# First group of the second layer's scans: its preparation spread over four more PSUM banks, and ScalarE's table loads moved

## The chip, the core and the metric

The kernel runs on one core of a Trainium2 chip. Five engines work side by side, each with an instruction queue of its own that it executes in order: TensorE (PE, matrix products; PEld is its weight load), VectorE (DVE), ScalarE (ACT, copies and functions from tables), GpSimd (POOL), and SyncE (SP), whose queue here issues transfers. They wait for one another by semaphores. Data lie in SBUF (128 partitions); TensorE writes to PSUM, which has eight banks of 512 float32 per partition. The metric is the time of one execution on the device in microseconds (us), the median of several runs.

## The reference

Two layers of the same build are applied to an image of 64 x 64 pixels with 96 channels. Each adds to x the output of a group norm, a projection to 2 x 192 channels (x_val and the gate z), a 3 x 3 depthwise convolution with silu, four selective scans with 16 states per channel along four pixel orders, a layer norm, the gate and a projection back. Cut to what matters, with the second layer's scan:

```python
xz = x @ in_proj_w.T;  xin, z = split(xz)
xc = silu(depthwise_conv3x3(xin) + conv_b)          # called u below
xs = stack([xf, xf[::-1], xf[o1], xf[o2]])          # four orders of the pixels
x_dbl = einsum('bkdl,kcd->bkcl', xs, x_proj_weight)
dts = einsum('bkrl,kdr->bkdl', x_dbl[:, :, :6], dt_projs_weight)
Bs, Cs = x_dbl[:, :, 6:22], x_dbl[:, :, 22:]
A = -exp(A_logs)
delta = softplus(dts + delta_bias)
def step(h, t):                                     # over 4096 pixels
    h = h * exp(d_t[..., None] * A) + (d_t * u_t)[..., None] * B_t[:, :, None, :]
    y = einsum('bkdn,bkn->bkd', h, C_t)
    return h, y
y = ys + u * D
y = layernorm(sum of the four, back in pixel order) * silu(z)
return y @ out_proj_w.T
```

The first layer's scan is written with cumulative sums, and its state is negligible some rows away from the image's border.

## The kernel before

The 4096 pixels of a channel lie in two halves over the 128 partitions: `u[T]` and `y[T]` (T = 0, 1, 2) are tiles of 128 x 2048, in which partitions 0 to 63 hold one half of the pixels of 64 channels and partitions 64 to 127 the other half. A *chunk* c is 512 columns of such a tile, that is 1024 pixels.

Each layer runs through the same stages. `head` (from L1005 on) computes the statistics of the group norm (`gst`, Ln at L1034 and Exp at L1035 on ScalarE), normalizes x (`xn`, L1040), projects it (`in`, copied to `pad` at L1051), runs the nine taps of the convolution on VectorE (`acc`, L1099 and L1101) and the silus on ScalarE (L1082 for the gate `sz`, L1103 for `u`). `scan_weights` is called ahead of `head`: it loads the projection weights (`xw`), those of delta (`dwb`) and log A (`ab`) over SP's queue, and computes `am` = -exp(log A) and half of it, with two exponents on ScalarE (L218) and two products on VectorE (L219, L220) for each pair of directions. The buffers of pair 0 have one copy for both layers.

In the first layer `near_scans` handles the pixels near the border, then reads a flag that says whether the rest can be left out. A branch (L1231) on it skips `far_scans`; in the profiled execution it was skipped. Its part up to the scans is prepared by TensorE, ScalarE and VectorE in turn (`nu`, `npj`, `npd`), and its transfers are `nC`, `ncb` and `ndu` on SP and `dt`, `S` on ScalarE's queue.

In the second layer `scans` does the work. There are 16 groups (two pairs of orders, two directions, four chunks). Each has 24 units: three tiles T by eight state pairs m. For each unit ScalarE computes a = exp(delta x A) (`stage_a`), TensorE makes b, which holds B times delta u, in PSUM, VectorE runs the scan h over 1024 pixels (`stage_s`), POOL multiplies by C (`stage_c`, hc), and TensorE adds the product up over the states (`stage_r`, ys). For even m, b comes from a selection of B's rows by TensorE (`stage_B`, selh, bank pair "b0") that VectorE multiplies by du (`stage_b`); for odd m it comes from products bT of transposed delta u and transposed B made by ScalarE, which TensorE transposes back (`stage_t`, "b1").

`prelude(k)` lists the preparation of group k as steps with a slot in units, group k's own first unit being slot 24. `project(h)` projects half h of the chunk to 124 rows (B three times, the six rows of each delta, C) as `pj`; `projected(h)` copies them to `xd` and takes B in bfloat16 (B3), and `less_part` and `next_part` subtract that from the rest and take the next two parts, so that three bfloat16 parts make up B. `rows` writes C to DRAM, from where `fetch_c` spreads its rows (cb). `tokens_B` transposes B (tB, copied to BT). `delta(T)` makes softplus: a product pd, then on ScalarE su = |pd|, sp = relu, w = exp(-su), ln = log(1+w), pd = 1 + w, then four VectorE steps (from group 1 on only the first, the other three on POOL) which leave delta in sp and delta times u in su. `spread(T)` copies both over SP's queue to the layout of the scan (dt, du). `tokens_du(e)` transposes su (tu, copied to duT), and `product` makes bT.

All PSUM tiles of the prelude share one bank, tag "v"; the other seven are "y0", "y1", "y2" (ys, one each), "b0" and "b1" (two each). So each step of the prelude that takes a bank waits until the one before it is read. The steps with a time below zero, all of group 0's and those of group 1's with a slot below 0, are issued ahead of the loop, sorted by time over both groups. Until the loop begins a scheduler may rearrange them; from `pinned` on the order written is kept. Calls to `tc.keep_in_program_order` pin single instructions, the table loads among them.

`tail` (from L1137 on) takes the four chunks from the last to the first through `centre` (mean by TensorE, subtraction on VectorE, Square on ScalarE), `scale` (variance by TensorE, Ln at L1159 and Exp at L1160, four VectorE operations g) and `project`, one chunk behind the other.

All operations of `scans` are recorded at L646, the line of its helper, and are told apart by their tiles.

Of the kernel before, what the change touches and what calls it, by code (L numbers as in the profile page):

```python
# [8 lines left out]
F32 = mybir.dt.float32  # L9
# [11 lines left out]
NS = 16  # L21
# [22 lines left out]
def two_ss2d_layers(  # L44
# [132 lines left out]
    def scan_weights(l):  # L177

        xw, dwb, am = [], [], []
        D = 1 + l
        for p in range(1 + l):
            lp = 2 * l + p
            w = swp.tile([128, 2, 3, NC], F32, tag=f"xw{p}", name=f"xw{lp}")
            v = swp.tile([128, 2, 3, 128], F32, tag=f"dwb{p}", name=f"dwb{lp}")
            e = swp.tile([128, 2, 3, NS + 1], F32, tag=f"ab{p}", name=f"ab{lp}")
            a = swp.tile([128, 2, 2, 3, NP], F32, tag=f"am{p}", name=f"am{lp}")
            nc.vector.memset(v[96:128, 0:D], 0.0)
            for d in range(D):  # L190
                r = slice(NB + RK * d, NB + RK * d + RK)
                rr = slice(RK * d, RK * d + RK)
                hi = slice(64 * d, 64 * d + 64)
                c0 = NB + 2 * RK + NS * d
                for half in HALF:
                    for to, of in ((slice(0, NC - NS), slice(0, NC - NS)), (slice(NC - NS, NC), slice(c0, c0 + NS))):
                        nc.sync.dma_start(
                            out=w[half, d, 0:2, to],
                            in_=xpw[lp, :, d, of].rearrange("(b p) c -> p b c", b=2),
                        )  # L200
                        nc.sync.dma_start(out=w[half, d, 2, to], in_=xpw[lp, hi, 2, of])
                    nc.sync.dma_start(
                        out=v[r, d, 0:2, half], in_=dtw[lp, rr, d, :].rearrange("r (b p) -> r b p", b=2)
                    )
                    nc.sync.dma_start(out=v[r, d, 2, half], in_=dtw[lp, rr, 2, hi])
                    for b, (of, q) in enumerate(((HALF[0], d), (HALF[1], d), (hi, 2))):
                        nc.sync.dma_start(
                            out=v[NC : NC + 1, d, b, half],
                            in_=alb[lp, of, q, NS : NS + 1].rearrange("p o -> o p"),
                        )  # L210
                    nc.sync.dma_start(
                        out=e[half, d, 0:2, :],
                        in_=alb[lp, :, d, :].rearrange("(b p) n -> p b n", b=2),
                    )
                    nc.sync.dma_start(out=e[half, d, 2, :], in_=alb[lp, hi, 2, :])

            for h, half in enumerate(HALF):
                nc.scalar.activation(a[half, 0, 0:D], e[half, 0:D, :, h:NS:2], AF.Exp)  # L218
            nc.vector.tensor_scalar_mul(a[:, 1, 0:D], a[:, 0, 0:D], -0.5)  # L219
            nc.vector.tensor_scalar_mul(a[:, 0, 0:D], a[:, 0, 0:D], -1.0)  # L220
            xw.append(w)
            dwb.append(v)
            am.append(a)
        return xw, dwb, am

    def row_of(rows, m, dst):

# [12 lines left out]
    def near_scans(weights):  # L240

        xw, dwb, am = (v[0] for v in weights)
        WN = 4 * NEAR
        with ExitStack() as sc:
            once = sc.enter_context(tc.tile_pool(name="near", bufs=1))
# [87 lines left out]
                once.tile([128, 3, 2, 2 * NEAR], F32, name=f"n{nm}") for nm in ("dt", "du", "S")  # L335
            )
            load_exp_ln()
            for T in range(3):
                nc.scalar.activation(w[:, T], ps[:, T], AF.Abs)
                nc.vector.tensor_scalar_max(v[:, T], ps[:, T], 0.0)  # L340
# [170 lines left out]

    def far_scans(weights):

        xw, dwb, am = (v[0] for v in weights)
        with ExitStack() as sc:
            pre = sc.enter_context(tc.tile_pool(name="fpre", bufs=1))
            mn = sc.enter_context(tc.tile_pool(name="fmn", bufs=2))
# [112 lines left out]
    def scans(weights):  # L630
# [1 line left out]

        xw, dwb, am = weights
        pinned = []

        class Ordered:
# [15 lines left out]
        with ExitStack() as sc:  # L654
# [2 lines left out]
            pps = sc.enter_context(tc.tile_pool(name="pps", bufs=1, space=PSUM))  # L657
            dram = sc.enter_context(tc.tile_pool(name="dram", bufs=3, space=DRAM))
            load_exp_ln()
            carry = pre.tile([128, 3, NP], F32, name="carry")  # L660
            PER = 3 * NP
            LAG = 3
# [3 lines left out]
            xd = pre.tile([128, TC], F32, name="xd")  # L666
            dve.memset(xd[96:128], 1.0)

            def spare(name):

                return pps.tile([128, HT], F32, tag="v", name=name)

            def views(t, c):

# [12 lines left out]
            def prelude(k):  # L687
# [3 lines left out]
                me = state[k]  # L691
                add_engine = pool if k else dve

                def turn(T):

                    t = pre.tile([128, HT // 2], F32, tag="turn", name=f"turn{k}_{T}")
                    v = views(u[T], c)[1][0]
                    t3 = t.rearrange("p (r w) -> p r w", w=HW)
                    act.copy(t3, v)
                    act.copy(v[:, :, ::-1], t3)  # L700

                def project(h):
                    ps = me["ps"] = spare(f"pj{k}_{h}")
                    for T in range(3):
                        pe.matmul(
                            ps[0:NC], xw[p][HALF[h], d, T, :], chunk(u[T], c)[HALF[h]],
# [1 line left out]
                        )  # L708

                def projected(h):  # L710
                    act.copy(xd[0:NC, halves[h]], me["ps"][0:NC])
                    if h == 0:
                        me["B3"] = pre.tile([NB, TC], BF16, tag="B3", name=f"B3{k}", bufs=3)
                    act.copy(me["B3"][:, halves[h]], me["ps"][0:NB])

                def less_part(h):
                    pe.matmul(
                        me["ps"][0:NB], less, me["B3"][:, halves[h]],  # L720
                        start=False, stop=True, skip_group_check=True,
                    )

                def next_part(part, h):
                    q = slice(0, 64 - 32 * part)
                    act.copy(me["B3"][q, halves[h]], me["ps"][q])

                def rows():
                    me["C"] = dram.tile([NS, TC], F32, tag="C", name=f"C{k}")
# [35 lines left out]
                def delta(T):  # L765

                    def begin():
                        ps = me["pd", T] = spare(f"pd{k}_{T}")
                        for h, half in enumerate(HALF):
                            pe.matmul(  # L770
                                ps[half], dwb[p][96 : NC + 1, d, T, half],
# [53 lines left out]
                    steps += [(-17 + T, lambda T=T: turn(T)) for T in range(3)]  # L825
                for h in range(2):
                    o = -13 + 3 * h
                    steps += [
                        (o, lambda h=h: project(h)),
                        (o + 1, lambda h=h: projected(h)), (o + 1, lambda h=h: less_part(h)),  # L830
                        (o + 2, lambda h=h: next_part(0, h)), (o + 2, lambda h=h: less_part(h)),
                        (o + 3, lambda h=h: next_part(1, h)),
                    ]
                steps += [
                    (-9, rows), (-6.8, tokens_B), (-5.95, tokens_B_out),
# [127 lines left out]
            def stage_y(j):  # L963
# [6 lines left out]
                        act.copy(view, f(ps))  # L970

            steps = [
                (PER * (k - 1) + slot, n, step)
                for k in range(len(GROUPS)) for n, (slot, step) in enumerate(prelude(k))
            ]
            steps.sort(key=lambda at: at[:2])
            while steps[0][0] < 0:
                steps.pop(0)[2]()

# [143 lines left out]
    def tail(l, w, xT):  # L1123
# [3 lines left out]
        with ExitStack() as sc:  # L1127
# [4 lines left out]
            for c in order:  # L1132
# [4 lines left out]
                    nc.sync.dma_start(out=t, in_=szd[l][T, :, HT * c : HT * (c + 1)])  # L1137
                cut = slice(TC * c, TC * (c + 1))
                nc.sync.dma_start(out=xT[:, cut], in_=xs[:, cut])
            load_exp_ln()  # L1140
            live = {}

            def centre(c):
# [9 lines left out]
            def scale(c):  # L1153
                cut = slice(HT * c, HT * (c + 1))
                pv = fps.tile([128, HT], F32, tag="v", name=f"v_{l}_{c}", bufs=1)
                for T in range(3):
                    nc.tensor.matmul(pv, pos, live[c, T], start=(T == 0), stop=(T == 2))
                rstd = fin.tile([128, HT], F32, tag="rstd", name=f"rstd{l}_{c}")
                nc.scalar.activation(rstd, pv, AF.Ln, bias=eps5)  # L1159
                nc.scalar.activation(rstd, rstd, AF.Exp, scale=-0.5)  # L1160
                for T in range(3):
# [158 lines left out]
```

## Time and profile before

| | us |
|---|---|
| median of 3 runs (1598.1 to 1598.31) | 1598.23 |
| the profiled execution | 1606.41 |
| its span, first to last instruction | 1604.6 |
| mean granted clock of TensorE | 0.874 of full |
| busy: VectorE / TensorE / ScalarE / POOL | 1392.8 / 1224.2 / 1211.8 / 1092.3 |
| first layer: head and convolution, near scans, tail | 0 to 97, to 194, to 241 |
| second layer: head and convolution, start of the scans, loop, tail | to 320, to 390, to 1556, to 1604.6 |

The times of all views are counted from the span's start. A line of the timeline has the start, the time from the first start to the last end, the engine, the line of the kernel, the operation with its output and inputs, how many instructions are merged in it, and in brackets the idle time of the engine before them with what ended it. A line of waits has the sum, the number and the longest one. A line of windows has the bounds and the length, busy time and number of instructions, TensorE's granted clock, and the share and rate of the transfers. The page's second part cuts the span into 40 slices, each digit being the busy share in tenths.

### The profile page before, as it was taken

How to read it: one execution, taken by the hardware profiler on the slowest of the kernel's cores; microseconds unless marked ns; L12 is line 12 of the kernel's file. 1: busy time of each engine (PE TensorE's matmuls, PEld its weight loads, DVE VectorE, ACT ScalarE, POOL GpSimd, SP SyncE). 2: the span in 40 equal slices, each digit the busy share in tenths (PEclk: the TensorE clock that was granted, in tenths of full speed). 3: DMA queues.
4: the chain of work that ended last, by engine and by line, in shares of the span. 5: the costliest groups of instructions: out<-in, count | busy, mean ns of one | idle time of the engine just before them, and what ended most of it. 6: DMA issues, size and time to landing. Idle time of an engine off the chain costs nothing.

```text
span 1604.6 us, 17094 instructions
## 1 busy us (share of the span) xinstructions
PE 1224.2 (76%) x5014; PEld 487.9 (30%) x5014; DVE 1392.8 (87%) x971; ACT 1211.8 (76%) x2463; POOL 1092.3 (68%) x577
## 2 busy tenths in 40 slices
PE   5452677157888888888878888888888888887768
PEld 3131422013333232333333333333333332322223
DVE  6946577923999999999999999999999999999976
ACT  2534156246898988989899989999898889897743
POOL 0022100003989899898989898998989898989860
PEclk8755598555999999999999899989999998999999
DMA  4304142040263443615262634526252626345323
GB/s 103 90 25 89 33 124 84 9 101 22 65 147 82 104 114 75 153 57 134 55 131 74 138 86 100 121 74 150 53 133 55 139 68 137 90 95 123 87 67 104
DMA packets 84308, 148.10 MB, mean 92 GB/s; under 512 B 31676, under 2 KB 35068, under 8 KB 84108
## 3 DMA queue, kind: packets, MB, share of 16 engines
q1 hardware_dynamic: 80428, 143.76, 37.4%
q10 hardware_dynamic: 3776, 3.15, 0.9%
q8 instruction: 41, 0.67, 0.2%
q14 instruction: 63, 0.52, 0.1%
HBM read 80.85 MB, written 12.13 MB: 58 GB/s over the span
## 4 chain that ended last, share of the span: by engine, by line
DVE 29%; issue 20%; ACT 14%; PE 12%; DMA 6%; SPq 4%; POOL 2%; DVEq 0%; ACTq 0%; POOLq 0%
DVE h L646 16%; DVE b L646 6%; ACT a L646 5%; SPq L646 4%; PE ys L646 4%; DVE acc L1101 4%; ACT bT L646 3%; DMA cb<-C 3%; PE pj L646 3%; PE b L646 2%; PE pd L646 2%; POOL hc L646 2%; DMA xT<-xs 1%; DMA du<-su 1%; DVE w L646 1%
## 5 line engine op out<-in xcount | busy, mean ns | idle before, releaser
L646 POOL TENSOR_TENSOR hc<-h,cb 128x1024 f32<-128x1024 f32 x384 | 903.3, 2367 | 251.6 <-DVE h L646 198.1
L646 DVE TENSOR_TENSOR_SCAN h<-a,carry,b 128x1024 f32<-128x1024 f32 x288 | 664.9, 2337 | 32.5 <-PE b L646 12.2
L646 ACT ACTIVATE a<-dt,am 128x1024 f32<-128x1024 f32 x384 | 438.7, 1143 | 100.3 <-DVE h L646 97.1
L646 PE MATMUL ys<-hc,fold 128*64 128x512 f32 x1536 | 432.8, 644 | 3.5 <-POOL hc L646 3.5
L646 ACT ACTIVATE bT<-duT,BT 128x192 f32<-128x192 f32 x1024 | 391.8, 445 | 11.0 <-PE b L646 8.9
L646 PE MATMUL b<-ident,bT 128*128 128x128 f32 x1536 | 226.3, 291 | 34.9 <-DVE h L646 29.6
L646 DVE TENSOR_TENSOR_SCAN h<-a,b 128x1024 f32<-128x1024 f32 x96 | 216.1, 2277 | 36.0 <-PE b L646 29.7
L646 DVE TENSOR_TENSOR b<-b,du 128x1024 f32<-128x1024 f32 x192 | 232.2, 1209 | 7.5 <-PE b L646 7.4
L646 PEld LDWEIGHTS b<-ident,bT 128*128 128x128 f32 x1536 | 178.2, 148 | 162.6 <-DVE h L646 99.6
L646 PE MATMUL b<-B,selh 96*128 96x512 bf16 x384 | 122.7, 402 | 94.9 <-DVE h L646 94.9
L646 PE MATMUL pj<-u,xw 64*124 64x512 f32 x192 | 102.0, 667 | 43.7 <-ACT u L1103 37.8
L646 PEld LDWEIGHTS ys<-hc,fold 128*64 128x64 f32 x1536 | 78.6, 139 | 140.4 <-issue 103.2
L1101 DVE SCALAR_TENSOR_TENSOR acc<-pad,v,acc 128x1052 f32<-128x1052 f32 x96 | 119.2, 1314 | 0.2
L646 PE MATMUL pd<-xd,dwb 29*64 29x512 f32 x192 | 63.9, 747 | 55.6 <-DVE w L646 49.2
L646 PEld LDWEIGHTS <-selh 96*128 96x128 bf16 x384 | 26.1, 98 | 227.0 <-DVE h L646 128.8
L646 PEld LDWEIGHTS pj<-u,xw 64*124 64x124 f32 x192 | 35.4, 199 | 110.1 <-issue 45.0
L646 PE MATMUL ys<-y,ident 128*128 128x512 f32 (+1 forms) x120 | 62.7, 628 | 0.0
L646 ACT CAST B<-pj 96x512 bf16<-96x512 f32 (+2 forms) x96 | 55.2, 575 | 5.5 <-PE pj L646 5.5
L646 POOL TENSOR_TENSOR ln<-ln,w 128x512 f32<-128x512 f32 x45 | 57.5, 1278 | 0.0
L646 POOL TENSOR_TENSOR su<-sp,u 128x512 f32<-128x512 f32 x45 | 57.5, 1278 | 0.0
L646 POOL TENSOR_TENSOR sp<-sp,ln 128x512 f32<-128x512 f32 x45 | 57.4, 1277 | 0.0
L646 DVE SCALAR_TENSOR_TENSOR w<-pd,w 128x512 f32<-128x512 f32 x48 | 32.1, 668 | 27.6 <-ACT pd L646 27.6
(166 smaller groups left out, 1110.9 us busy)
## 6 DMA issues: line engine op xcount, KB each, us to landing
cb<-C SPq DMA_DIRECT2D x256, 256.0 KB, 4.0
dt<-sp SPq DMA_DIRECT2D x192, 128.0 KB, 4.3
du<-su SPq DMA_DIRECT2D x192, 128.0 KB, 4.1
szd<-sz SPq DMA_DIRECT2D x24, 256.0 KB, 2.5
szt<-szd SPq DMA_DIRECT2D x24, 256.0 KB, 8.0
xT<-xs SPq DMA_DIRECT2D x8, 384.0 KB
xs<-xT SPq DMA_DIRECT2D x1, 1536.0 KB
xs<-xT SPq DMA_DIRECT2D x8, 192.0 KB
```

Source lines behind the costliest of these rows:

```text
L646: ins = op(*args, **more)
L1101: nc.vector.scalar_tensor_tensor(acc, src, wk, acc, ALU.mult, ALU.add)
```

## The change

Four things are edited.

The preparation of `am` becomes a function of its own, `decays`. It is called behind the table load of `near_scans` (for pair 0 of the first layer) and behind the one at the start of `scans` (for both pairs of the second layer), and its exponents are pinned.

In group 0 the five steps that take a bank get tags of their own: the two projections "y0" and "y1", the products of delta "y2", "b1" and "v". The later groups keep "v" for all.

In group 0 the taking of B's three parts is moved back by 9.5 slots, behind the first steps of delta; `projected` then only copies to `xd`. The steps ahead of the loop are issued group by group, group 0's before group 1's.

In `tail` the table load moves from the start to just ahead of the first Ln.

```diff
+    def decays(am):
+        for a, e, D in am:
             for h, half in enumerate(HALF):
-                nc.scalar.activation(a[half, 0, 0:D], e[half, 0:D, :, h:NS:2], AF.Exp)
+                tc.keep_in_program_order(
+                    nc.scalar.activation(a[half, 0, 0:D], e[half, 0:D, :, h:NS:2], AF.Exp)
+                )
             nc.vector.tensor_scalar_mul(a[:, 1, 0:D], a[:, 0, 0:D], -0.5)
             nc.vector.tensor_scalar_mul(a[:, 0, 0:D], a[:, 0, 0:D], -1.0)
+        return [a for a, e, D in am]
...
             load_exp_ln()
+            am = decays(weights[2])[0]
...
             load_exp_ln()
+            am = decays(weights[2])
...
+                tags = ("y0", "y1", "y2", "b1", "v") if k == 0 else ("v",) * 5
...
-                    ps = me["ps"] = spare(f"pj{k}_{h}")
+                    ps = me["pj", h] = spare(f"pj{k}_{h}", tags[h])
...
-                        ps = me["pd", T] = spare(f"pd{k}_{T}")
+                        ps = me["pd", T] = spare(f"pd{k}_{T}", tags[2 + T])
...
+                    late = 0 if k else 9.5
                     steps += [
                         (o, lambda h=h: project(h)),
-                        (o + 1, lambda h=h: projected(h)), (o + 1, lambda h=h: less_part(h)),
-                        (o + 2, lambda h=h: next_part(0, h)), (o + 2, lambda h=h: less_part(h)),
-                        (o + 3, lambda h=h: next_part(1, h)),
+                        (o + 1, lambda h=h: projected(h)),
+                        (o + 1 + late, lambda h=h: first_part(h)),
+                        (o + 1 + late, lambda h=h: less_part(h)),
+                        (o + 2 + late, lambda h=h: next_part(0, h)),
+                        (o + 2 + late, lambda h=h: less_part(h)),
+                        (o + 3 + late, lambda h=h: next_part(1, h)),
                     ]
...
-                (PER * (k - 1) + slot, n, step)
+                (PER * (k - 1) + slot, n, step, k)
...
-            steps.sort(key=lambda at: at[:2])
+            steps.sort(key=lambda at: (at[0] >= 0, at[0] < 0 and at[3], at[:2]))
...
-            load_exp_ln()
             live = {}
...
+                if c == order[0]:
+                    load_exp_ln()
                 nc.scalar.activation(rstd, pv, AF.Ln, bias=eps5)
```

## The prediction

> **What bounds the kernel now.** I read the page first, then ScalarE's and VectorE's timelines around the places that the diff touches, then what VectorE waited for and TensorE's granted clock. Page and waits:
>
> ```profile
> span 1604.6 us, 17094 instructions
> ...
> DVE  6946577923999999999999999999999999999976
> ```
> ```profile
> DVE h L646 <- PE b L646: 16.2, 14, 1.8
> DVE b L646 <- PE b L646: 6.5, 10, 0.8
> ```
>
> From slice 11 on VectorE is full: the scans of the second layer are its chain, and between 405 and 1550 us it waits some 24 us in all. So time is to be had ahead of the loop (its start, at 320 to 390 us, is slice 9 with the digit 2), in the layer tails, or not at all. The first layer's tail, and the link to the second layer's head:
>
> ```profile
> 205.43 1.28 ACT L1159 ACT_TABLE_LOAD   x1
> 206.73 0.69 ACT L1159 ACTIVATE rstd<-v,eps 128x512 f32<-128x512 f32 x1
> 207.43 1.28 ACT L1160 ACT_TABLE_LOAD   x1
> 208.73 0.63 ACT L1160 ACTIVATE rstd<-rstd 128x512 f32<-128x512 f32 x1
> ...
> 243.78 1.28 ACT L1034 ACT_TABLE_LOAD   x1 [12.88 <-issue]
> ...
> 245.35 1.28 ACT L1035 ACT_TABLE_LOAD   x1
> ```
> ```profile
> 225.71 1.42 DVE L1163 SCALAR_TENSOR_TENSOR g<-y,v,rstd 128x512 f32<-128x512 f32 x2 [2.85 <-ACT rstd L1160]
> ...
> 246.88 3.73 DVE L1040 TENSOR_SCALAR xn<-xT,gst 96x512 f32<-96x512 f32 x8 [3.71 <-ACT gst L1035]
> ```
>
> Every Ln and every Exp loads a table of its own, ten loads in this stretch, and VectorE waits behind some of them. The start of the scans:
>
> ```profile
> 342.16 0.69 DVE L646 SCALAR_TENSOR_TENSOR w<-pd,w 128x512 f32<-128x512 f32 x1 [21.79 <-ACT pd L646]
> ...
> 354.45 5.48 PE L646 MATMUL pj<-u,xw 64*124 64x512 f32 x6 [3.75 <-DVE w L646]
> ...
> 374.13 0.90 PE L646 MATMUL tu<-ident,su 128*128 128x128 f32 x3 [0.36 <-ACT BT L646]
> ...
> 383.94 2.29 DVE L646 TENSOR_TENSOR_SCAN h<-a,b 128x1024 f32<-128x1024 f32 x1 [23.90 <-PE b L646]
> ```
>
> Group 0's delta is ready at 356.6, but group 1's projection sits in the one bank "v" from 354.45 to 374.08, ahead of group 0's token transposes (tu). Unit 1's scan (h1) waits 23.90 us for them. The clock there:
>
> ```profile
> 100.00:105.00 5.00, 5.00 (x15) 0.50 0.00 0
> 105.00:110.00 5.00, 5.00 (x9) 0.50 0.00 0
> ```
>
> These are five-microsecond windows (TensorE busy, clock granted): matmuls of the form of pj (npj, 8.04 us without a gap from 102.10) ran at 0.50 to the end. So did all of 300 to 395 us.
>
> **The change part by part.** All terms are against the profiled execution: 1604.6 us of span, 1606.41 us in all; the median of the runs is 1598.23, 8.2 lower, and I take the same difference off it. What each engine executes, and in which order, I take from the two built kernels.
>
> *Decay preparation leaves the first head.* Four VectorE operations (am) go from the gapless convolution, where they cost 0.12, 0.11, 0.09 and 0.12 us start to start: -0.4. Their exponents took four loads with them (68.75, 70.31, 75.57, 78.30), but ScalarE next waited 9.91 us for VectorE: 0. In near_scans two exponents (0.25 each) now follow the load at 112.18; TensorE's npd releases ScalarE only at 115.49, so 2.02 us of idle cover 0.5, and VectorE's two products fit into its idle 4.71 us: 0. Were that cover gone, they would cost 0.5 + 0.3. The two loads at 150.40 and 153.62 go; VectorE waits there for ny from TensorE (2.46 us) and not for ScalarE: 0, bounded by -1.3. On SP the eight ab2 loads move behind nC, since ab's buffer is now freed at 114; the one ahead of ncb holds it by about 1 us, and ncb is read only at 147. The other seven end near 122, ahead of ndu at 128.72: 0. The am2 exponents ran in 28 us of idle: 0. The TensorLoad of the flag goes to the end of ScalarE's near work, which is followed by that idle: 0.
>
> *First tail.* One load stays at 205.43, nine go. The load between Ln and Exp of the first chunk held g: Exp ends at 208.07 instead of 209.36. One 0.6 us subtraction that ran in that gap now comes behind, so VectorE gains 0.7. From there it works without a gap to 222.85, now 222.1. The next chunk's Ln follows its last Square (ends 221.0), Exp ends at 222.4, g starts then instead of 225.71: 3.3. The 16 us that follow are VectorE alone (rstd of the last chunk is ready at 226.5, needed at 228.9). Then Ln and Exp of gst each lose a load, 2.6: together -5.9. The szt and xT transfers, issued from 194.51 to 206.82 with 8.0 us to landing, are in by 215 and not late: chunk 2's szt are issued by 198 and wanted at 215.
>
> Here a rule would change the sum. The row: the load at 205.43 lasts 1.28 us and the next activation starts 0.02 us after it. The Trainium skill (ScalarE: Activation LUTs, "What ACT_TABLE_LOAD costs") adds a drain of about 1.38 us to each, 2.66 us a switch. With that, five loads on the path would give 6.9 us more here, and the load of the last part 1.4 more of loss, the whole sum -16.8. The rows show no drain, so I take 1.28.
>
> *Start of the scans.* I use the times of before, as if the last u still came at 320.32. ScalarE: y to 321.50, table to 322.78, four new exponents (0.25 each) to 323.82, two copies to xd to 324.9, B's first parts to 325.9. TensorE (clock 0.50): both projections done by 324.0; then in its queue tB half 0.55, a pd half alone, tB half 0.55, less 0.6, a pd pair 1.97, two less 1.2, a pd pair 1.97, a pd half alone, b0 0.6, less 0.6. A pd half alone has no row; it lies between 0.99 (half of a pair's 1.97) and 1.97; I take 1.8, two matmuls at pj's 0.91. Sum 11.6: 324.45 to 336.1. ScalarE sends the first Identity (pd) at 333.9, so VectorE's first w is at 333.9 instead of 342.16 and dt leaves on SP at 336.1. ScalarE then stands 2.3 us for the last less; behind it wait su and sp of the other two tiles. From 336.15 its seven steps at 0.48 to 0.66 end at 340.6. VectorE's four operations (2.85) end at 343.45; the shared buffer of w frees at 342.0, so ScalarE's third w and pd end at 343.4, and VectorE's last four at 346.25 (before: 356.6). C0 is written at 325 and its rows asked for before dt needs SP; cb0_1's second half, now behind du0_2, leaves at 352.7 for a product on POOL at 363. POOL's order is as before.
>
> Then tu to the fourth duT: rows 374.13 to 381.22, 7.1, plus a2 (1.15), which now lies among them: 354.55. Behind it TensorE has group 1's first projection, 5.48, and only then the last transposes for unit 1, 0.69: h1 at 360.9, 23 us earlier. **What is late next** is group 1: unit 3's scan is queued behind w1_0, and w1_0 needs all of group 1's projection. Before, first to second half took 9.14 (354.45+5.48 to 369.07); now unit 3's transposes, which wait for h1, stand between: second projection done at 371.3. From there to BT1 5.0 (369.07 to 374.08), pd 2.0, ScalarE's steps to pd 4.95 (383.33 to 388.28): w1_0 at 383.3, h3 at 384.0 instead of 390.24: -6.2. From there on all queues have the order of before.
>
> The bounds of this term: pairs of pd that don't overlap across steps add 2 x 1.7, and semaphores perhaps 1: -2. Single halves at 0.99 take 1.6 off: -8. The second rule: the Trainium skill (TensorE: Matmul & The Clock Gate, "Part 1: The HAM clock gate") says that about 3.4 us of sustained work releases the full clock. TensorE is nearly gapless here from 354.6 to 371, so by the rule the second projection would take 2.84 (its row in the loop) and the term be about -11.5. The 8.04 us of npj at 0.50 speak against it.
>
> *Last tail.* The load ran at 1558.48, in a gap of 4.36 us. It now stands between the last Square (ends 1568.4) and Ln, and g at 1569.89 starts 1.25 later. VectorE has no gap from there to 1582.7: +1.25, bounds 0 and 1.28.
>
> Sum: -0.4 - 5.9 - 6.2 + 1.25 = -11.3. Profiled span 1593.3, median 1586.9.
>
> **Rivals.** (a) TensorE's clock opens during group 1's projections. For it: the pairs of halves and the transposes now lie closer together, and at 248 to 252 us four microseconds of paired halves opened it. Saved: 2.64 on one projection, 1.0 on pd, some 1.8 on the rest: 1581.5. (b) The first group's preparation is 4 us longer (pd halves not overlapping, which no row shows for different steps): 1591. (c) Group 1's chain takes all of the start's gain: ScalarE has nothing to lend while it also makes bT, so h3 comes at 390: 1593 to 1596. (d) Slower: the loop's waits for b grow. They occur where the clock drops to 0.50 for a few microseconds (1.83 at 484.10), and a loop that starts at another moment may meet such drops otherwise. It decides from 24 to 39 us of waits on, eight more of 1.83; for it speaks the loop's mean clock of 0.95, against it the unchanged order and three runs within 0.2 us: 1602. That the loads do not go is excluded, since the built kernel has 15 fewer on the path taken.
>
> **How the numbers follow.** The forecast holds 0.62, (a) 0.13, (b) 0.14, (c) 0.06, (d) 0.05. The range goes from (a) to just past (b) with a microsecond or two for the loop: 1580.5 to 1592.5, leaving out (c), (d) and the edges. 0.2% is 3.2 us, about what a measurement of this kernel can tell from none; below 1595.0 lie the first three and half of (c): 0.92 faster, 0.04 the same, 0.04 slower.
>
> **What would show it.** In the first tail one table load, and gst's two steps back to back; g after Exp without 2.85 us of wait. h1 some 25 us after the first issue of dt, then a wait of VectorE ahead of w1_0 of about 16 us. h3 at 64 us after the last u (70 before). In the last tail a load between Square and Ln. I am wrong if w1_0 follows h2 at once, if pj runs at 0.47 a matmul there, or if the waits for b in the loop are far from 24 us.

## The result and the profile after

The changed kernel takes 1584.28 us (median of four runs, 1582.61 to 1585.94); runs of the kernel before on the same chip gave a median of 1598.16. The ratio is 0.9913 (95% interval 0.9896 to 0.9931). On another chip, later, it was 0.9923 (0.9894 to 0.9953). Forecast: 1586.9, that is 11.3 us less than before; on the first chip the medians differ by 13.9. The times of one kernel spread over several microseconds, some over 20, so the terms are read from the profiles, from one fixed instruction to the next, and the times only say whether the sum fits.

The page of the changed kernel:

```profile
span 1584.1 us, 17071 instructions
...
DVE  6956488935998999999999999999999999999976
```

VectorE's slices 9 and 10, which read 2 and 3 before, are now 3 and 5: the scans start earlier and still not at once. ScalarE's timeline over the first layer's tail and the second layer's norm (start, duration, operation; in brackets the idle time before it and what ended it):

```profile
200.91 1.82 ACT L1170 ACTIVATE sq<-y 128x512 f32<-128x512 f32 x3 [0.69 <-DVE y L1168]
202.75 1.28 ACT L84 ACT_TABLE_LOAD   x1
204.04 0.69 ACT L1180 ACTIVATE rstd<-v,eps 128x512 f32<-128x512 f32 x1
204.76 0.63 ACT L1181 ACTIVATE rstd<-rstd 128x512 f32<-128x512 f32 x1
...
238.52 0.26 ACT L1054 ACTIVATE gst<-pv,eps 96x1 f32<-96x1 f32 x1 [14.95 <-DMA xs<-xT]
238.81 0.20 ACT L1055 ACTIVATE gst<-gst 96x1 f32<-96x1 f32 x1
```

VectorE in the same stretch:

```profile
219.65 1.42 DVE L1184 SCALAR_TENSOR_TENSOR g<-y,v,rstd 128x512 f32<-128x512 f32 x2
...
233.74 1.28 DVE L1202 TENSOR_TENSOR xT<-o,xT 96x512 f32<-96x512 f32 x2 [1.04 <-PE o L1196]
...
239.04 3.73 DVE L1060 TENSOR_SCALAR xn<-xT,gst 96x512 f32<-96x512 f32 x8 [1.15 <-ACT gst L1055]
```

One load is left, behind the last Square (sq). In the kernel before, this load (L84) ran at 150.40, still among the near scans; their next tanh (L431) loaded its own table at 153.62, so the tail came to its first Ln without the table meant for it. That each Ln and each Exp then loads one of its own, and not one for both, is seen there; why, no run shows. The 2.85 us of wait ahead of the third chunk's g are gone, the wait ahead of xn is 1.15 us and was 3.71, and at 233.74 VectorE meets a new wait, 1.04 us for TensorE's o. The start of the scans, all engines:

```profile
312.72 2.14 PE L653 MATMUL pj<-u,xw 64*124 64x512 f32 x4 [1.85 <-ACT u L1123]
...
326.33 0.69 DVE L653 SCALAR_TENSOR_TENSOR w<-pd,w 128x512 f32<-128x512 f32 x1 [9.72 <-ACT pd L653]
...
346.32 5.48 PE L653 MATMUL pj<-u,xw 64*124 64x512 f32 x6
...
352.46 2.29 DVE L653 TENSOR_TENSOR_SCAN h<-a,b 128x1024 f32<-128x1024 f32 x1 [10.32 <-PE b L653]
...
374.67 0.69 DVE L653 SCALAR_TENSOR_TENSOR w<-pd,w 128x512 f32<-128x512 f32 x1 [16.41 <-ACT pd L653]
375.28 2.27 DVE L653 TENSOR_TENSOR_SCAN h<-a,b 128x1024 f32<-128x1024 f32 x1
```

In the kernel before, the last u and the scan of unit 3 (h3) were these:

```profile
319.17 1.15 ACT L1103 ACTIVATE u<-acc,v 128x1024 f32<-128x1024 f32 x1 [1.59 <-DVE acc L1101]
...
390.24 2.28 DVE L646 TENSOR_TENSOR_SCAN h<-a,b 128x1024 f32<-128x1024 f32 x1
```

The last u of the changed kernel ends at 312.67. The first w follows 13.66 us later (21.84 before), the scan h1 of unit 1 39.79 (63.62 before), h3 (at 375.28) 62.61 (69.92 before). The 23.90 us of wait ahead of h1 have become 10.32 there and 16.41 ahead of w1_0, group 1's first w. In the last tail the load stands between Square and Ln:

```profile
1545.32 1.83 ACT L1170 ACTIVATE sq<-y 128x512 f32<-128x512 f32 x3 [0.69 <-DVE y L1168]
1547.16 1.28 ACT L84 ACT_TABLE_LOAD   x1
1548.45 0.69 ACT L1180 ACTIVATE rstd<-v,eps 128x512 f32<-128x512 f32 x1
...
1549.90 1.41 DVE L1184 SCALAR_TENSOR_TENSOR g<-y,v,rstd 128x512 f32<-128x512 f32 x2 [3.42 <-issue]
```

In the kernel before, it ran ahead of them:

```profile
1558.48 1.28 ACT L84 ACT_TABLE_LOAD   x1
...
1566.59 1.82 ACT L1151 ACTIVATE sq<-y 128x512 f32<-128x512 f32 x3 [0.69 <-DVE y L1149]
...
1569.89 1.41 DVE L1163 SCALAR_TENSOR_TENSOR g<-y,v,rstd 128x512 f32<-128x512 f32 x2 [2.14 <-issue]
```

From the end of the last Square to g it takes 2.75 us (1.48 before).

The spans of the two profiles differ by 20.5 us. Laid out between fixed instructions (acc is the convolution's operation, nus the first copy of the near scans, and the memset of dwb VectorE's first operation behind them):

| stretch | before | after | difference |
|---|---|---|---|
| start to the first acc of layer 1 | 32.15 | 31.43 | -0.72 |
| convolution of layer 1, to nus | 64.83 | 64.80 | -0.03 |
| near scans, to the memset of dwb | 97.61 | 97.05 | -0.56 |
| to the first g | 14.87 | 12.22 | -2.65 |
| first g to xn | 37.42 | 33.54 | -3.88 |
| xn to the end of the last u of layer 2 | 73.44 | 73.63 | +0.19 |
| last u to h3 | 69.92 | 62.61 | -7.31 |
| h3 to the end of the last scan (the loop) | 1162.94 | 1158.95 | -3.99 |
| last scan to the first g of the last tail | 16.71 | 15.67 | -1.04 |
| that g to the end | 34.71 | 34.20 | -0.51 |

The loop's -3.99 stands in no term of the forecast, and the order of the work from h3 on is the same in both. The first profile of before is of an execution 8 us above the median of its kernel. Which rows belong to the change is what the experiments had to settle.

### The profile page after: what moved, and what is told of

It is laid out like the page before. It is cut to its first block, busy times and chain, and to the rows that moved or that the text cites. A ratio compares the mean times of both kernels' runs of the same rounds, so it can differ in the third digit from the quotient of the medians.

```text
span 1584.1 us, 17071 instructions
## 1 busy us (share of the span) xinstructions
PE 1216.4 (77%) x5014; PEld 483.7 (31%) x5014; DVE 1395.5 (88%) x971; ACT 1191.5 (75%) x2448; POOL 1092.8 (69%) x577
## 4 chain that ended last, share of the span: by engine, by line
DVE 32%; issue 21%; PE 13%; ACT 11%; DMA 4%; POOL 4%; SPq 3%; DVEq 0%; ACTq 0%; POOLq 0%
DVE h L653 18%; DVE b L653 7%; PE ys L653 4%; ACT a L653 4%; DVE acc L1121 4%; PE b L653 3%; POOL hc L653 3%; SPq L653 3%; PE pj L653 2%; ACT bT L653 2%; PE pd L653 2%; DMA du<-su 1%; DMA szt<-szd 1%; DVE w L653 1%; DMA cb<-C 1%
## 5 line engine op out<-in xcount | busy, mean ns | idle before, releaser
L653 PE MATMUL b<-ident,bT 128*128 128x128 f32 x1536 | 222.7, 289 | 31.8 <-DVE h L653 27.5
L653 ACT CAST B<-pj 64x512 bf16<-64x512 f32 (+2 forms) x96 | 55.1, 576 | 7.8 <-PE pj L653 7.8
L1123 ACT ACTIVATE u<-acc,v 128x1024 f32<-128x1024 f32 x12 | 13.8, 1146 | 59.3 <-DVE acc L1121 59.3
```

Of the source, the lines that this page charges most:

```text
L653: ins = op(*args, **more)
L1123: nc.scalar.activation(u[b][:, cut].rearrange("p (c r w) -> p c r w", c=2, w=HW), room[:, :, :, 0:HW], AF.Silu, bias=v[:, b, V_CB : V_CB + 1],
```

## The experiments

The theory after the result: the change is worth its three terms (first tail, start, last tail), the banks carry the start, group 1 is what is late next, and the rest of the table is the granted clock. The rivals: the loads or the order by groups carry the gain; the loop is faster because of the change; group 1 isn't what limits the start.

### Only the tail's load moved

The kernel before, with one edit:

```diff
@@ tail
-            load_exp_ln()
             live = {}
@@ scale
+                if c == order[0]:
+                    load_exp_ln()
                 nc.scalar.activation(rstd, pv, AF.Ln, bias=eps5)
```

> The kernel before with one edit: the table load of both tails moves ahead of the first Ln. By the steps of the prediction: first tail 0.7 + 2.6 + 2.6 us off, last tail 1.25 on, so -4.6 us, some 1593.6. Up to the last u of the second layer the profile gains 5.9 us, and the loop from unit 3's scan to the last scan keeps its length, 1162.9 us in the profile of before. The rival says that what went beyond the forecast came from the loop's waits for b: then the loop's length moves by up to 4 us here too, although no instruction in it is changed.

Measured: 1592.85 us (12 runs, 1587.86 to 1608.29), ratio 0.9987 (0.9958 to 1.0015). By the times alone nothing is shown. By the profile, first g to xn is 32.56 us (37.42 before), last Square to g 2.77 (1.48), last u to h3 69.90 (69.92). So the first tail's gain and the last tail's loss come from this edit alone, and it leaves the start as it was. The loop took 1152.46 us, 10.5 less than in the first profile of before, though nothing in it is edited; that a loop can move without an edit is what I had named as the rival's sign.

### The tables without the new preparation

The changed kernel with

```diff
-                tags = ("y0", "y1", "y2", "b1", "v") if k == 0 else ("v",) * 5
+                tags = ("v",) * 5
...
-                    late = 0 if k else 9.5
+                    late = 0
...
-            steps.sort(key=lambda at: (at[0] >= 0, at[0] < 0 and at[3], at[:2]))
+            steps.sort(key=lambda at: at[:2])
```

> The changed kernel without the new preparation of group 0 (one bank, B's parts and order of the groups as before); decays and table loads as in the change. By the steps: -0.4 (convolution) - 5.9 (first tail) + 1.0 (the four exponents now ahead of the first copy to xd, with no longer path to hide them) + 1.25 (last tail) = -4.0 us, some 1594.2. If the preparation of am in the first head cost more than its four products on VectorE, it comes out below the run with the tail's load alone. Length of the loop as in the run before it.

Measured: 1595.21 us (1590.15 to 1606.9), ratio 0.999 (0.9966 to 1.0015). h1 comes 64.80 and h3 71.10 us after the last u, 1.18 later than before: the four exponents of the decays, which now stand at the head of the scans, cost that there. The tables' sum, then, is small: some five microseconds from the first tail, 1.2 lost at the start and 1.3 in the last tail.

### The preparation without the tables

The changed kernel with `decays` called for each layer where it stood before, in `scan_weights` (its exponents no longer pinned), and the tail's load at its old place. Cut to the calls:

```diff
@@ scan_weights
             am.append((a, e, D))
+            am[-1] = decays(am[-1:])[0]
@@ near_scans
-            am = decays(weights[2])[0]
+            am = weights[2][0]
@@ scans
-            am = decays(weights[2])
+            am = weights[2]
@@ tail
+            load_exp_ln()
             live = {}
@@ scale
-                if c == order[0]:
-                    load_exp_ln()
```

> The changed kernel with am and the tail's table load back at their old places: only the new preparation of group 0 is left. By the steps: -6.2 - 1.0 (no exponents ahead of the copies to xd) = -7.2 us, some 1591.0. Unit 3's scan starts 62.7 us after the last u is ready (before 69.9). If the loop's waits for b give more than 2 us of their own, the time is below 1589 and the loop shorter than 1161 us in the profile.

Measured: 1588.69 us (1585.33 to 1593.35), ratio 0.9935 (0.9912 to 0.9958). h1 at 38.76, h3 at 61.58 after the last u: 8.3 us earlier than before, 1.03 earlier than in the changed kernel. First g to xn is 37.42 us as before, last Square to g 1.48. The preparation carries the larger part of the change, and the decays give 1.0 of it back. The time is below 1589 and the loop took 1155.53 us, which together I had named as the sign that the loop's waits for b gain something of their own; the next run but one shows that this sign can't be read.

### Layer 2's load back at the head of the tail

The changed kernel with

```diff
@@ tail
+            if l:
+                load_exp_ln()
             live = {}
@@ scale
-                if c == order[0]:
+                if c == order[0] and not l:
```

> The changed kernel, with the second layer's last table load back at the tail's start and the first layer's left where the change put it. By the steps this gives back the 1.25 us of the last tail: 1583.0 against the changed kernel's 1584.3, and in the profile g starts 1.5 us after the last Square of its pair, not 2.75. The rival: TensorE's means end last there, and the time stays at 1584.3.

Measured: 1585.81 us (1581.0 to 1587.58), ratio 0.9911 (0.9889 to 0.9933). Against the changed kernel's 0.9913 no difference can be told. The profile has 1.48 us from the last Square to g, where the changed kernel has 2.75; h3 at 62.61 in both. The term is real, and too small for the times.

### The kernel before, profiled again

No edit.

> The kernel before, unchanged, profiled a second time. Theory (the program's start is repeatable to some hundredths of a microsecond, and what varies from execution to execution is the granted clock in the loop and in the products m of the two tails): from the last u to h3 69.9 us again, wait ahead of h1 23.9; but the stretch from h3 to the end of the last scan differs from the 1162.94 of the first profile, and lies near 1155, as the loops of the experiments do (1152.5 to 1158.7). Rival (the loop of before is longer than that of the changed kernel for a reason of the program): 1161 to 1164 again.

Measured: one run, 1597.07 us, span 1595.2. VectorE's timeline:

```profile
383.59 2.29 DVE L646 TENSOR_TENSOR_SCAN h<-a,b 128x1024 f32<-128x1024 f32 x1 [23.89 <-PE b L646]
...
389.89 2.28 DVE L646 TENSOR_TENSOR_SCAN h<-a,b 128x1024 f32<-128x1024 f32 x1
```

The last u ends at 319.98, so h1 comes 63.61 and h3 69.91 us after it, as in the first profile to 0.01 us. The loop took 1153.92 us in place of 1162.94: the same program, 9.02 us apart. What VectorE waited for between 405 and 1530 us, in this execution (total, times, longest):

```profile
DVE h L646 <- PE b L646: 9.9, 13, 1.9
DVE b L646 <- PE b L646: 3.1, 5, 0.8
```

and in the changed kernel's:

```profile
DVE h L653 <- PE b L653: 14.0, 18, 2.4
DVE b L653 <- PE b L653: 4.5, 7, 0.9
```

So the loop's -3.99 in the table lies within what one program does from execution to execution, and no effect of the change on the loop is shown; by this second profile the loop of before is even 5.0 shorter than the changed one's. What such a wait stands behind is seen in windows of the changed kernel (TensorE busy, granted clock, share of the DMA engines, GB/s):

```profile
446.00:449.40 3.40, 1.32 (x6) 0.94 0.07 14
449.40:452.80 3.40, 3.40 (x8) 0.50 0.00 0
452.80:456.20 3.40, 3.40 (x14) 0.56 0.00 0
456.20:459.60 3.40, 3.40 (x14) 1.00 0.29 86
```

and in VectorE's timeline there:

```profile
456.21 2.35 DVE L653 TENSOR_TENSOR_SCAN h<-a,carry,b 128x1024 f32<-128x1024 f32 x1 [1.77 <-PE b L653]
```

For some seven microseconds the clock is at half, and behind them VectorE waits 1.77 us. Summed in windows of one microsecond (a window at 0.50 counts in full), the clock was at half for 124 us of the first loop of before, 105 us of the second, 128 of the changed kernel's, and 102 to 135 in the nine experiments' loops, whose lengths go from 1152.46 to 1164.73. Over all 13 profiles, the two kernels' repeats among them, the two quantities correlate with 0.86, at 0.28 us of loop for each microsecond at half clock. This is a correlation: no run that sets the clock by itself was tried.

### The changed kernel again

No edit.

> The changed kernel, unchanged, on the same chip as the version below. From the last u to h1 39.8 and to h3 62.6; the loop 1155 to 1160; 1583 to 1587.

Measured: 1589.28 us (1586.4 to 1590.25), ratio 0.9923 (0.9894 to 0.9953). h1 at 39.79, h3 at 62.60 after the last u, last Square to g 2.77, first g to xn 32.77 (33.54 in the first profile), the loop 1157.85. The median is 2 us above the range expected; the ratio's interval overlaps the first one's.

### Which part of the preparation carries it: one bank, old order, B first

Three kernels, each the changed one with one line turned back:

```diff
# all of group 0 in one bank
-                tags = ("y0", "y1", "y2", "b1", "v") if k == 0 else ("v",) * 5
+                tags = ("v",) * 5
```
```diff
# the steps of both groups sorted together
-            steps.sort(key=lambda at: (at[0] >= 0, at[0] < 0 and at[3], at[:2]))
+            steps.sort(key=lambda at: at[:2])
```
```diff
# B's parts at once
-                    late = 0 if k else 9.5
+                    late = 0
```

> The changed kernel with all of group 0's steps in the one bank v; the order by groups stays. Theory (the banks carry the gain): the first w comes 23 us after the last u (13.7 in the changed kernel; 23.0 where only the tables were moved), h1 about 51 and h3 about 74, which is later than the 71.1 where only the tables were moved: the order by groups alone costs 3. Rival (the order carries a good part): h3 under 67 after the last u.

> The changed kernel with the steps of both groups sorted together, as before; group 0 keeps its banks and its order of dt and B. Group 1's projections and its parts of B then stand ahead of group 0's transposes, one after the other in the bank v. Theory (with the banks, the order by groups no longer pays for unit 1 what it costs unit 3): h1 later, about 50 us after the last u (39.8), no wait ahead of w1_0, h3 about 57 (62.6): some 5 us faster than the changed kernel, 1578 to 1581. Rival (the order by groups carries the gain): h3 at 69 to 71 as before, 1591 to 1594.

> The changed kernel with B's parts of group 0 made at once, behind the copy of each half, and not behind dt. In the built order that moves two steps of TensorE and a few copies of ScalarE by one to two places. Theory: first w 14 to 15 us after the last u (13.7), h3 62.6 to 63.8 after it: that dt comes first is worth 1.2 us at most. Rival (B's parts hold dt up): first w over 17, h3 over 65.

Measured, in us after the last u, with the run that moved only the tables as the fourth corner (it also takes B's parts at once, which the other three do not):

| | first w | h1 | h3 |
|---|---|---|---|
| one bank, groups together (tables only) | 23.03 | 64.80 | 71.10 |
| one bank, by groups | 23.04 | 50.38 | 73.19 |
| banks, groups together | 13.66 | 53.57 | 59.87 |
| banks, by groups (the changed kernel) | 13.66 | 39.79 | 62.61 |
| the same, B's parts first | 17.17 | 41.15 | 63.97 |

The banks take 11.2 us (groups together) or 10.6 (by groups) off h3. The order by groups adds 2.1 (one bank) or 2.7 (banks) to it, though it brings h1 14 us forward: it moves the wait from unit 1 to unit 3 and makes it longer. The 10.6 and the 2.7 are each the work of one edit; the 11.2 and the 2.1 hold B's order too. Times: one bank 1594.82 (one run); groups together 1584.07 (1582.76 to 1585.65), ratio 0.9905 (0.9876 to 0.9934), where 1578 to 1581 was expected; B first 1590.42 (one run). The 2.7 us don't come out in the times, and the old order's h1 and h3 are some 3 us later than I had expected. Its timeline on TensorE and VectorE:

```profile
338.43 5.48 PE L653 MATMUL pj<-u,xw 64*124 64x512 f32 x6 [7.25 <-DVE w L653]
...
347.82 5.48 PE L653 MATMUL pj<-u,xw 64*124 64x512 f32 x6 [0.67 <-ACT B L653]
...
368.17 2.29 DVE L653 TENSOR_TENSOR_SCAN h<-a,b 128x1024 f32<-128x1024 f32 x1 [24.10 <-PE b L653]
```

The first projection waits until VectorE's third w has read pd, which lies in bank v too, as group 0's transposes tB and tu do; I had freed the bank after ScalarE's reads.

That dt comes first is worth 3.5 us at the first w and 1.4 at h3. That is 0.2 more than the upper bound I had set, and the mechanism is the one I had as the rival. ScalarE's timeline with B first:

```profile
325.37 0.63 ACT L653 ACTIVATE w<-su 128x512 f32<-128x512 f32 x1
328.93 0.57 ACT L653 CAST B<-pj 32x512 bf16<-32x512 f32 x1 [2.93 <-PE pj L653]
329.41 0.72 ACT L653 ACTIVATE ln<-w,one 128x512 f32<-128x512 f32 x1
```

The last copy of B stands between two steps of the softplus, and waits 2.93 us for a product that TensorE has behind its pairs of pd.

### Banks for group 1's projections too

```diff
-                tags = ("y0", "y1", "y2", "b1", "v") if k == 0 else ("v",) * 5
+                tags = {0: ("y0", "y1", "y2", "b1", "v"), 1: ("y0", "y1", "v", "v", "v")}.get(k, ("v",) * 5)
```

> The changed kernel, but group 1's two projections get the banks y0 and y1 in place of the one bank v, so TensorE does both ahead of group 0's token transposes. Theory (group 1's chain is what is late next, because its halves pass through one bank one after the other): h1 stays within 1.5 us of 39.8 us after the last u, VectorE's 16.41 us of wait ahead of w1_0 fall under 4, h3 comes 46 to 49 us after the last u (62.6 in the changed kernel), and the time falls by 14 to 16 from 1584.3, to 1568 to 1571. Rival 1 (something behind group 1, its delta's transfers or GpSimd, is late anyway): h3 still 58 to 63 after the last u, 1580 to 1585. Rival 2 (h1 pays for it, since 11 us of projections now stand ahead of the transposes): h1 50 and h3 57 after the last u, 1578.

Measured: 1574.53 us (six runs, 1567.4 to 1579.12; 1568 to 1571 was expected), ratio 0.9845 (0.9813 to 0.9877). h1 at 43.22, h3 at 51.15 after the last u, the wait ahead of w1_0 0.83 us. Group 1's chain was what was late; the gain at h3 is 11.5 us and not 14 to 16, and h1 paid 3.4. Where, is seen on the three engines:

```profile
326.59 3.77 PE L653 MATMUL pj<-u,xw 64*124 64x512 f32 x4
...
330.99 0.57 ACT L653 CAST B<-pj 32x512 bf16<-32x512 f32 x1 [4.55 <-PE pj L653]
...
338.93 0.58 ACT L653 COPY xd<-pj 124x512 f32<-124x512 f32 x1 [3.24 <-PE pj L653]
...
355.51 2.29 DVE L653 TENSOR_TENSOR_SCAN h<-a,b 128x1024 f32<-128x1024 f32 x1 [6.18 <-PE b L653]
```

Group 0's last step of B is queued on TensorE behind group 1's first projection, and ScalarE, which waits for it, holds up the softplus of group 0's third tile.

### The same, with the places written out

With the two banks kept, group 1's projections (P_AT), copies to xd (X_AT) and parts of B (B_AT) get slots in group 0's list and are held in that order, as is group 0's last less_part (`ours[5]`); and layer 2's load stands at the head of the tail. Cut to what matters (`ours` is the list of these steps that was added to `steps`):

```diff
+            P_AT, X_AT, B_AT = (6.9, 18.2), (18.25, 18.4), ((22.1, 22.2, 22.3, 22.4, 22.5), (22.6, 22.7, 22.8, 22.9, 22.95))
...
+                def kept(step):
+                    def run():
+                        pinned.append(True)
+                        step()
+                        pinned.pop()
+
+                    return run
...
+                    if k == 0 and h == 1:
+                        ours[5] = (6.8, kept(ours[5][1]))
+                        ours[6] = (6.85, ours[6][1])
+                    if k == 1:
+                        at = (P_AT[h], X_AT[h]) + tuple(B_AT[h])
+                        ours = [(a - PER, kept(f), 0) for a, (_, f) in zip(at, ours)]
...
-                (PER * (k - 1) + slot, n, step, k)
+                (PER * (k - 1) + slot, n, step, *(early or [k]))
...
+            if l:
+                load_exp_ln()
...
-                if c == order[0]:
+                if c == order[0] and not l:
```

> Group 1's projections in the banks y0 and y1 as in the run with two banks for it, but with their place written out: both behind group 0's last step of B and ahead of its token transposes, the copies to xd behind group 0's softplus, group 1's parts of B behind group 0's token transposes; and layer 2's last table load back at the head of the tail. In the run with two banks ScalarE stood 4.55 us for a step of B that was queued behind a projection, and 3.24 us for the second projection, both ahead of group 0's third tile, whose su ended 33.5 us after the last u (25.9 in the changed kernel). Theory (those two stalls are what that run paid): third su at 26 to 27, h1 39 to 41, h3 46.5 to 48.5 after the last u (43.2 and 51.2 there), 1 us more from the tail: 4 us faster than the 1574.5 of that run, 1568 to 1572, 14 us under the changed kernel. Rival (ScalarE's copies of group 1 push the products of group 0 instead): h1 43 or later, h3 51 to 53, 1573 to 1576.

Measured: 1572.06 us (five runs, 1567.26 to 1573.74), ratio 0.9811 (0.9785 to 0.9837): 28 us under before by the medians, 30 by the ratio, 17 under the changed kernel's second measurement, which is of the same chip. It has the lowest median of this study. Third su 24.99, h1 35.05, h3 45.56 us after the last u; last Square to g 1.48. h1 is 4 us and h3 1 us better than the lower ends of what was expected. The timeline shows a part of the reason:

```profile
326.25 6.32 PE L653 MATMUL pj<-u,xw 64*124 64x512 f32 x12
...
346.03 2.29 DVE L653 TENSOR_TENSOR_SCAN h<-a,b 128x1024 f32<-128x1024 f32 x1 [6.54 <-PE b L653]
...
356.54 2.28 DVE L653 TENSOR_TENSOR_SCAN h<-a,b 128x1024 f32<-128x1024 f32 x1
```

Both projections together take 6.32 us, where one took 5.48. The profiled execution itself had the longest loop of all (1164.73 us, 135 at half clock), which ate what the start gained beyond the run with two banks; by the medians it is 2.5 us faster than that one, which ran on another chip, and the intervals of the two ratios overlap: by the times, the two can't be told apart.

## Why the prediction was right, and where it was off

*Convolution, -0.4: wrong, it was -0.03.* From the first acc to nus it is 64.83 us in both profiles of before and 64.80 in both of the changed kernel. The step that failed is "where they cost 0.12, 0.11, 0.09 and 0.12 us start to start". Without am the stretch from the first of two accs to what follows the second is 2.70 us (32.24 to 34.94), with am in it 2.69 (32.96 to 35.65): am filled a gap between two operations that was there anyway. Before and after on VectorE:

```profile
32.96 1.32 DVE L1101 SCALAR_TENSOR_TENSOR acc<-pad,v,acc 128x1052 f32<-128x1052 f32 x1
34.19 0.17 DVE L219 TENSOR_SCALAR am<-am 128x24 f32<-128x24 f32 x1
...
35.65 0.77 DVE L1099 TENSOR_SCALAR acc<-pad,v 128x1052 f32<-128x1052 f32 x1
```
```profile
32.24 2.66 DVE L1121 SCALAR_TENSOR_TENSOR acc<-pad,v,acc 128x1052 f32<-128x1052 f32 x2
34.94 0.77 DVE L1119 TENSOR_SCALAR acc<-pad,v 128x1052 f32<-128x1052 f32 x1
```

I had read the time from a start to the next start as the price, and should have compared a stretch that has no am in it. The near scans, which I had put at 0, took 97.61 and 96.74 us in the two profiles of before and 97.05 and 97.50 in those of the changed kernel: no difference between the programs can be told there.

*First tail, -5.9: right.* From the last Square ahead of it to the first g it is 4.05 us before and 2.77 after, in both profiles of each; from that g to xn 37.42 and 37.36 before, 33.54 and 32.77 after. Sum: -5.1 to -5.9. The lower value has the new 1.04 us of wait for TensorE's o, which I hadn't named as what is late next; the second profile hasn't got it. TensorE's clock was at half for 6.8 us from 227.1 us on in the first profile, and for 3.4 from 231.2 in the second. The rest of the -2.65 in the table, 1.37, goes with the clock, which came to full 3.1 us behind the memset of dwb, and 5.9 behind it in the first profile of before, while TensorE made the means m. The second profiles fit: 13.80 us from the memset to the first g in before, with the clock full 3.7 us behind it, and 13.55 in the changed kernel, with 5.8.

*Start of the scans, -6.2: right in mechanism, measured -7.31.* First w forecast 13.6 after the last u, measured 13.66; third su 25.9 and 25.95; h1 40.6 and 39.79; w1_0 63.0 and 62.00; h3 63.7 and 62.61. The term that was too large, by 1.1 us, is TensorE's stretch from the third su to the end of group 1's second projection: forecast 51.0 after the last u, measured 49.93. Of the unknown costs, the pd half alone took 1.96 us (317.40 in the trace; I took 1.8), and a pair across steps 1.97, so that rival (b) fell. "What is late next is group 1" was right; what I didn't ask is whether the order by groups helps at all: at h3 it costs 2.7.

*Last tail, +1.25: right.* 1.48 us became 2.75. Some 0.4 us came back between g and the end (34.71 in both profiles before, 34.20 and 34.34 after), which no term had, and whose cause is open. The -1.04 ahead of g in the table is the 1.28 of the load and a shorter drop of the clock: in the changed kernel's second profile, where it was at half for 6.8 us there as in both of before (3.4 in the first), the stretch is 18.00 us against 16.71.

Put together, the parts that repeat give -0.03 - 5.1 to -5.9 - 7.3 + 1.3 - 0.4, that is -11.5 to -12.3, against -11.3. That the sum comes so close is in part luck: 0.4 at the convolution and up to 0.8 in the first tail were forecast and not gained, 1.1 at the start and 0.4 at the end were gained and not forecast, and these nearly cancel. The first chip's medians differ by 13.9, the second's by 10.4. What lies between these and the terms I put down to the clock in the loop and ahead of the tails' first chunks; for the runs without a profile that is not shown.

*The rivals.* (a) TensorE's granted clock stayed at 0.50 from 312 to 380 us in the changed kernel. (c) h3 did move. (d) The loop's waits for b, between 405 and 1530 us, were 18.5 us, with 22.7 in the first profile of before and 13.0 in the second: the place was right, but the size differs more between two executions of one program than between the versions. My sign for it, waits far from 24 us, could therefore not be read from one profile.

*The two rules that I weighed.* The moved load is 1.28 us long, the Ln behind it starts 0.01 us after it, and the path grew by 1.27 to 1.29 us. The Trainium skill ("ScalarE: Activation LUTs", section "What ACT_TABLE_LOAD costs") adds a drain of about 1.38 us to each switch; the measurement shows none, and decides.

With banks for group 1, TensorE was busy for 19.86 of the 20 us from 320 to 340 and stayed at 0.50 throughout. In the version with the places written out it worked without a gap from 315.15, and the clock was released at about 331.4, after 16 us:

```profile
330.00:331.00 1.00, 1.00 (x6) 0.50 0.97 205
331.00:332.00 1.00, 1.00 (x5) 0.79 0.96 211
332.00:333.00 1.00, 0.89 (x3) 1.00 0.96 201
```

The Trainium skill ("TensorE: Matmul & The Clock Gate", section "Part 1: The HAM clock gate") says that about 3.4 us of sustained work releases the full clock. These rows don't agree with that: being busy without a gap, as the profile counts it, wasn't enough.

## What to carry to other kernels

When a chain is shortened, the gain ends where the next chain in the queue of the same engine takes over; ask for that one before the edit, and give it the same resource (here two PSUM banks), which was worth nearly as much again as the whole change. An order that finishes one group first can be worse for the group behind it (2.7 us at h3 here, too little for the times to show): measure where the second group starts, not only the first. Where single runs differ by more than the terms, measure from one fixed instruction to the next in two profiles of the same program; what repeats to 0.01 us can be put down to the program, and what moves by 9 us can't.

## What I had not expected of the hardware

Products of two halves whose inputs lie in partitions 0 to 63 and 64 to 127 run side by side, if they stand next to each other in TensorE's queue: 2.14 us for four of pj at half clock (312.72 in the changed kernel), where two of one half take 2.07 (320.37 in before); and twelve took 6.32 us where six took 5.48. In the run with banks for group 1, where a step of B and one of b stood between the halves, they took their full time. Part of the 6.32 is the released clock of its last 1.2 us, as the windows above show.

Two operations that follow each other on the same tile leave a gap on VectorE that small ones can use: that is argued from the convolution's 2.70 and 2.69 us, and not tested by itself.
